# Cross attention in a fused decoder: two layer norms cut into small pieces, and the next row's preparation laid out in thirteen groups

## The chip, the cores and the metric

The kernel runs on one core of a Trainium2 chip. A core has five engines that work side by side, each on its own queue of instructions in a fixed order: TensorE (PE) does matrix products, with its weight loads shown apart (PEld); VectorE (DVE) and ScalarE (ACT) do elementwise work and empty the accumulators (PSUM) that PE writes; GpSimd (POOL) does elementwise work too; SyncE (SP) issues the DMA transfers. An instruction that waits holds up everything behind it on its own queue. The metric is the device time of one execution in microseconds, the median of some runs. The profile is of one execution and has a time of its own.

## The reference

A decoder of two layers on x of 8 batch rows x 512 positions x 256 channels, all float32. Six sublayers follow one another (self attention, cross attention and a local transformer; then quantized attention, media attention and a mixture of experts), each added to its own input's residual. The change touches the second, cross attention with 16 heads of 16 channels:

```python
x = x + _L0_xattn_ref(_layernorm(x), ctx, ctx, adj, mask, Wq, bq, Wk, bk, Wv, bv, Wo, bo)
# in it, per batch row and head: softmax(q k^T / 4 + adj, masked) v, then Wo
...
x = x + _L0_ffn_ref(_layernorm(x), ...)
```

A batch row has 512 queries and 512 keys. `_layernorm` takes mean and variance over the 256 channels of each position and gives (x - mean) / sqrt(var + 1e-5). Two of these norms matter here: the one ahead of cross attention (called x_ln below) and the one ahead of the local transformer (lt_ln), which is worked out at the end of cross attention.

## The kernel before, in words

**Stages.** `fast_stages` runs the sublayers in order on one core. While a stage runs, an `Ahead` object lets the next stage's preparation be written into the program a few pieces at a time (`ahead.step`). The whole of x (`self.x`, 128 partitions x 32 tiles x 256 channels) stays on chip; a batch row is four tiles (`NST`).

**Cross attention** (`stage_cross_attention`, L1476 to L1750) runs a loop over 128 steps, 16 to a batch row; I number rows and steps from 0. A step covers one group of heads and one tile of 128 keys. `scores` (L1640) puts 4 x 2 small products into two PSUM tiles `sc`, of which there are three; `soften` (L1657) takes the exponential of each on ACT (L1663) and multiplies it on DVE by a table `x_share` that holds mask and exp(adj) (L1664); the result is `x_e`, of which there are six buffers, two per step. `weigh` (L1669), two steps behind, multiplies x_e with the values into the PSUM tile `po`, of which there is one. At every fourth step po is copied out by ACT (L1685), its sums of weights go through DRAM and back (`inverted`, L3162), DVE takes their reciprocal (L3174), and a DMA spreads them over the partitions (`x_wide`), where POOL multiplies (L1696).

**The next row's preparation** (`prepare`, L1540) is given out piece by piece with the steps of the current row. In the program's order of before: `load` (three DMA transfers: context, mask, and zeros for a later stage) and `norm` at step 1; `keys` twice at step 2 (K, evicted by DVE at L1601); four `values` (V, evicted by ACT at L1610), with the four `share` pieces (DVE, L1560), at steps 3 to 8; two `turn` (T, transposes, L1578, evicted by ACT at L1581) at steps 9 and 10; two `queries` (Q, evicted by two ACT instructions at L1594) at steps 11 and 12. K, V, T and Q and the final projection all pass through one PSUM tile, `pj`, of which there is one. `norm` is x_ln: per tile bn_stats and bn_aggr (L143, L144), then the mean, the variance and 1/sqrt by a guess and three Newton steps (`rsqrt`, L1455: 12 small instructions together), then four normalizing instructions into `x_xn`, of which there is one (L157), and x + bias on POOL (L1570).

**Work due later.** `Background` holds thunks with a due step; `later.tick(2)` runs at most two of those due in each step. By it the row's projection `project_out` (P, L1709) comes some twelve steps into the next row, four pieces, each a product into pj and an addition into x on DVE (L1717). The fourth also sends the row to DRAM (`away`, L1720) and does lt_ln as a whole: statistics, 12 root instructions, and four normalizing instructions in place on x (lt_ln's L157, LT below).

**What sets the order on the queues.** The kernel is written with Tile, which takes the program's order as a priority and plans a queue for each engine: an instruction is placed when its inputs and its buffers are there, by the planner's own reckoning, and of several that are ready the earliest in the program goes first. So a piece of low priority can stand far ahead of its place in the program when its inputs and buffers are free early. `together` (L1448) keeps the four products of a group side by side on PE.

Of the kernel before, what the change touches and what calls it, by code (L numbers as in the profile page):

```python
# [27 lines left out]
F32 = mybir.dt.float32  # L28
F32R = mybir.dt.float32r
BF16 = mybir.dt.bfloat16  # L30
I32 = mybir.dt.int32
# [3 lines left out]
ALU = mybir.AluOpType  # L35
# [4 lines left out]
P = 128  # L40
B, S, C = 8, 512, 256
NST = S // P
NT = B * NST
EPS = 1e-5
# [12 lines left out]
class Decoder:  # L57
# [1220 lines left out]
class FastDecoder(Decoder):  # L1278
# [177 lines left out]
    def rsqrt(self, pool, out, v, tag):  # L1456
# [4 lines left out]
        for _ in range(3):  # L1461
            nc.vector.scalar_tensor_tensor(t, out, -0.5, out, ALU.mult, ALU.mult)
            nc.vector.tensor_tensor(t, t, v, ALU.mult)
            nc.vector.scalar_tensor_tensor(out, t, 1.5, out, ALU.add, ALU.mult)

    def load_cross_attention(self):
        w = self.weights()
        names = "x_wqT", "x_wkT", "b_wvT", "b_woT"
        return [self.load_w(w, 512 * i, self.t[n]) for i, n in enumerate(names)]
# [6 lines left out]
    def stage_cross_attention(self, ahead):  # L1476
# [6 lines left out]
        nc, t = self.nc, self.t  # L1483
# [41 lines left out]
        bias = self.alloc(pool, [P, C], F32, "x_bias", bufs=1)  # L1525
# [8 lines left out]
        held = {}  # L1534
# [5 lines left out]
        def prepare(b):  # L1540

            d = held[b] = {"v": v_pad[b % 2]}
            own = (first, second)[b % 2]

            def load():
                d["ctxT"] = self.alloc(first, [P, 2, S], F32, "x_ctxT")
                nc.sync.dma_start(
                    d["ctxT"], t["ctxT"].rearrange("(k p) n -> p k n", p=P)[:, :, b * S : (b + 1) * S]
                )
                d["mask"] = self.alloc(first, [P, NST, S], I32, "x_mask", bufs=1)  # L1550
                nc.sync.dma_start(d["mask"], t["x_maskT"][b].rearrange("(k p) q -> p k q", p=P))
                nc.sync.dma_start(
                    self.slots[b * CAP : (b + 1) * CAP, :].rearrange("(p r) c -> p r c", p=P),
                    empty.unsqueeze(1).broadcast_to([P, CAP // P, self.WIDE]),
                )

            def share(k):
                if k == 0:
                    d["share"] = self.alloc(own, [P, NST, S], F32, f"x_share{b % 2}", bufs=1)
                nc.vector.scalar_tensor_tensor(  # L1560
                    d["share"][:, k, :], d["mask"][:, k, :], 0.0, adj[:, k, :], ALU.not_equal, ALU.mult
                )

            def norm():
                x = self.x[:, b * NST : (b + 1) * NST, :]
                stats = self.ln_stats(first, lambda i: [x[:, i, :]], NST, "x_ln")
                d["xn"] = self.alloc(first, [P, NST, C], F32, "x_xn", bufs=1)
                for i in range(NST):
                    self.normalize(d["xn"][:, i, :], x[:, i, :], stats, i)
                nc.gpsimd.tensor_tensor(x, x, bias.unsqueeze(1).broadcast_to([P, NST, C]), ALU.add)  # L1570
                d["xnT"] = self.alloc(first, [P, 2, S], F32, "x_xnT", bufs=1)
                d["q"] = self.alloc(own, [P, 2, 2, S], F32, f"x_q{b % 2}", bufs=1)
                d["k"] = self.alloc(own, [P, 2, S], F32, f"x_k{b % 2}", bufs=1)

            def turn(c):
                ps = self.pj()
                for i in range(NST):
                    nc.tensor.transpose(  # L1578
                        ps[:, i * P : (i + 1) * P], d["xn"][:, i, c * P : (c + 1) * P], self.ident
                    )  # L1580
                nc.scalar.copy(d["xnT"][:, c, :], ps)  # L1581

            def project(wt, src, g):
                ps = self.pj()
                for k in range(2):
                    nc.tensor.matmul(
                        ps, wt[:, k, g * P : (g + 1) * P], src[:, k, :], start=(k == 0), stop=(k == 1)
                    )
                return ps

            def queries(g):
                ps = project(wq, d["xnT"], g)
                for e in range(2):
                    nc.scalar.activation(  # L1594
                        d["q"][:, e, g, :], ps, AF.Identity,
                        bias=qb[:, 2 * e + g : 2 * e + g + 1], scale=qsc[:, e : e + 1],
                    )

            def keys(g):
                ps = project(wk, d["ctxT"], g)  # L1600
                nc.vector.tensor_scalar(d["k"][:, g, :], ps, bk[:, g : g + 1], None, ALU.add)  # L1601

            def values(i):
                ps = self.pj()
                for k in range(2):
                    nc.tensor.matmul(
                        ps[:, :C], d["ctxT"][:, k, i * P : (i + 1) * P], wv[:, k, :],
                        start=(k == 0), stop=(k == 1),
                    )
                nc.scalar.copy(  # L1610
                    d["v"][:, i, :, 1:17], ps[:, :C].rearrange("p (h d) -> p h d", d=16)
                )

            yield load
            yield norm
            for g in range(2):
                yield lambda g=g: keys(g)
            for i in range(NST):
                yield lambda i=i: values(i)
                yield lambda i=i: share(i)  # L1620
            for c in range(2):
                yield lambda c=c: turn(c)
            for g in range(2):
                yield lambda g=g: queries(g)

        second = None
        for thunk in prepare(0):
            thunk()
            yield
        yield Ahead.MAIN  # L1630

        with self.tc.tile_pool(reuse_waits="tile", name="xa", bufs=2) as pool, self.tc.tile_pool(
# [24 lines left out]
            def soften(n):  # L1657
                b, rest = divmod(n, 16)
                kt = rest % 4
                d = held[b]  # L1660
                for p in range(2):
                    ex = self.alloc(pool, [P, 2, 512], F32, "x_e", bufs=6)
                    nc.scalar.activation(ex, d["e"][rest][p], AF.Exp)  # L1663
                    nc.vector.tensor_tensor(  # L1664
                        ex, ex, d["share"][:, kt, :].unsqueeze(1).broadcast_to([P, 2, 512]), ALU.mult
                    )
                    d["e"][rest][p] = ex
# [41 lines left out]
            def project_out(b, i):  # L1709
                ps = self.pj()  # L1710
                for g in range(2):
                    nc.tensor.matmul(
                        ps[:, :C], held[b]["oT", g][:, i * P : (i + 1) * P], wo[:, g, :],
                        start=(g == 0), stop=(g == 1),
                    )
                x = self.x[:, b * NST + i, :]
                nc.vector.tensor_tensor(x, x, ps[:, :C], ALU.add)  # L1717
                if i == NST - 1:
                    rows = self.x[:, b * NST : (b + 1) * NST, :]
                    nc.sync.dma_start(self.away[b], rows)  # L1720
                    stats = self.ln_stats(pool, lambda i: [rows[:, i, :]], NST, "lt_ln")
                    for i in range(NST):
                        self.normalize(rows[:, i, :], rows[:, i, :], stats, i)

            n = 16 * B
            ready = None
            for i in range(n + 2):
                if i < n:
                    if i % 16 == 0:
                        for thunk in ready or ():  # L1730
                            thunk()
                        ready = prepare(i // 16 + 1) if i // 16 + 1 < B else iter(())
                    scores(i)
                    soften(i)
                if i >= 2:
                    weigh(i - 2)

                for _ in range((0, 2, 2, 1, 2, 1, 2)[i % 16] if i % 16 < 7 else 1):
                    thunk = next(ready, None)
                    if thunk is not None:  # L1740
                        thunk()
                later.tick(2)
                if i == 1:
                    ahead.step()
                if i == n - 14:
                    early.close()
                if i >= n - 12:
                    ahead.step(3)
# [1696 lines left out]
```

## Time and profile before

| What | Value |
|---|---|
| Time, median of 3 runs | 3174.21 us (3169.55 to 3178.64) |
| The profiled execution's own time | 3162.05 us |
| Its span, first to last instruction | 3160.1 us |
| Granted TensorE clock over the span | 0.973 |
| Busy over the span: PE, DVE, ACT, POOL | 2877.0, 2166.9, 1154.0, 408.7 us |
| First x_e of cross attention starts, last ends | 207.6, 707.9 us |
| Matmuls of sc (L1652) and po (L1679) | 1024 of 662 ns, 1024 of 620 ns, several at a time |
| x_e: exponential on ACT (L1663), product on DVE (L1664) | 256 of 1026 ns, 256 of 1253 ns |

Groups of instructions are named by line, engine, operation, and output<-inputs by the program's names. Of an instruction, the idle time of its engine just before it and what ended it (its releaser) is given. Matmul ends are modelled, so the starts on PE's timeline are the safer numbers. A line in a helper (L143, L144, L157 and L1455 to L1464) serves several norms; the tile's name tells which.

### The profile page before, as it was taken

Reading aid. Unit: us, or ns where it says so; the run is one execution under the profiler, and the core shown is the slowest. Engines: PE = TensorE matmul, PEld = TensorE weight load, DVE = VectorE, ACT = ScalarE, POOL = GpSimd, SP = SyncE. Lnnn points to the kernel's source line nnn. Section 1 sums busy time; section 2 is a strip of 40 time slices with the busy share of each in tenths; the row PEclk is TensorE's granted clock in tenths of the full one; section 3 lists DMA queues with packets and bytes.
Section 4 is the critical chain, followed back from the end, with each engine's and each line's share of the span. In section 5 each row is a group of like instructions: output and inputs, shape, how many; then the busy total and the mean of one; then the engine's idle time right before and its main releaser. Section 6 shows DMA issues by size and latency. Waiting matters only on the chain. (4 is left out here: it accounts for less than half of the span.)

```text
span 3160.1 us, 40243 instructions
## 1 busy us (share of the span) xinstructions
PE 2877.0 (91%) x14929; PEld 1485.8 (47%) x14944; DVE 2166.9 (69%) x4962; ACT 1154.0 (37%) x1607; POOL 408.7 (13%) x389
## 2 busy tenths in 40 slices
PE   8998888877998989999988989998796999997998
PEld 5642222224555556655555546654444233333665
DVE  7458888887788795357788798558787766566110
ACT  2146556653434431123434431113353444342111
POOL 1111000000011010000101111111201122222111
PEclk9999999989999999999999999999997999998999
DMA  7011111111000001001000011001332122213331
GB/s 237 1 53 44 54 57 48 32 24 51 16 21 22 19 27 42 0 1 35 22 15 21 22 44 61 15 12 60 95 127 94 41 79 103 75 64 103 102 138 59
DMA packets 130695, 168.73 MB, mean 53 GB/s; under 512 B 51760, under 2 KB 79665, under 8 KB 128442
## 3 DMA queue, kind: packets, MB, share of 16 engines
q1 hardware_dynamic: 126394, 154.48, 15.6%
q0 software_dynamic: 4096, 11.59, 1.0%
q8 instruction: 119, 1.95, 0.3%
q14 instruction: 86, 0.70, 0.1%
HBM read 113.12 MB, written 47.50 MB: 51 GB/s over the span
## 5 line engine op out<-in xcount | busy, mean ns | idle before, releaser
L1812 PE MATMUL pj<-w,la_hT 128*128 128x512 f32 x720 | 345.3, 612 | 23.9 <-DVE la_v L1817 21.9
L1664 DVE TENSOR_TENSOR x_e<-x_e,x_share 128x1024 f32<-128x1024 f32 x256 | 309.1, 1253 | 25.1 <-ACT x_e L1663 24.3
L1663 ACT ACTIVATE x_e<-sc 128x1024 f32<-128x1024 f32 x256 | 249.7, 1026 | 147.9 <-PE sc L1652 145.5
L2817 ACT ACTIVATE ma_e<-sc,ma_bias 128x1024 f32<-128x1024 f32 x128 | 142.4, 1114 | 198.8 <-PE sc L2812 185.5
L1812 PEld LDWEIGHTS pj<-w,la_hT 128*128 128x128 f32 x720 | 129.5, 191 | 167.0 <-issue 119.0
L3188 POOL TENSOR_TENSOR la_oT<-la_o,x_wide 128x512 f32<-128x512 f32 x64 | 96.8, 1523 | 790.6 <-DMA x_wide<-invs 654.6
L2825 DVE TENSOR_TENSOR ma_esum<-ma_esum,ma_e 128x1024 f32<-128x1024 f32 x96 | 122.8, 1280 | 91.6 <-ACT ma_e L2817 90.9
L1933 ACT ACTIVATE la_e<-la_e 128x1024 f32<-128x1024 f32 (+1 forms) x128 | 121.4, 951 | 175.2 <-DVE la_e L1929 175.2
L2146 ACT ACTIVATE lf_gate<-pj,lf_b 128x512 f32<-128x512 f32 (+1 forms) x82 | 56.3, 687 | 338.1 <-PE pj L2125 327.1
L1679 PE MATMUL po<-x_e,x_v 128*32 128x512 f32 x1024 | 140.1, 620 | 37.2 <-DVE x_e L1664 34.1
L2125 PE MATMUL pj<-lf_hnT,w 128*128 128x512 f32 (+1 forms) x368 | 171.9, 595 | 1.2 <-DVE lf_hid L2151 1.1
L1929 DVE TENSOR_TENSOR la_e<-sc,la_mask 128x1024 f32<-128x1024 f32 (+1 forms) x128 | 138.3, 1081 | 38.8 <-PE sc L1922 38.8
L1652 PE MATMUL sc<-x_q,x_k 32*128 32x512 f32 x1024 | 159.2, 662 | 0.3 <-ACT x_e L1663 0.2
L2125 PE MATMUL sc<-lf_hnT,w 128*128 128x512 f32 x336 | 158.0, 592 | 0.0
L2197 PE MATMUL po<-w,lf_hid 128*128 128x256 f32 x640 | 148.9, 379 | 0.2 <-DVE x L2207 0.2
L1988 PE MATMUL pj<-w,la_oT 128*128 128x256 f32 x512 | 124.4, 389 | 23.4 <-ACT la_qkT L1858 12.6
L2812 PE MATMUL sc<-ma_qT,ma_kT 64*128 64x512 f32 x512 | 145.2, 644 | 0.0
L2151 DVE SCALAR_TENSOR_TENSOR lf_hid<-sc,lf_b,lf_gate 128x512 f32<-128x512 f32 x70 | 52.4, 748 | 126.3 <-PE sc L2125 126.3
L2835 PE MATMUL po<-ma_e,ma_v 128*64 128x512 f32 x512 | 138.1, 618 | 0.0
L1940 PE MATMUL po<-la_e,la_v 128*64 128x256 f32 (+1 forms) x1024 | 129.1, 374 | 6.4 <-ACT la_o L1962 6.3
L1922 PE MATMUL sc<-la_qkT 64*128 64x256 f32 (+1 forms) x1024 | 132.6, 378 | 1.3 <-DVE la_e L1929 1.3
L1819 ACT ACTIVATE la_sq<-pj 128x512 f32<-128x512 f32 x120 | 71.4, 595 | 156.2 <-PE pj L1812 155.9
(491 smaller groups left out, 5264.5 us busy)
## 6 DMA issues: line engine op xcount, KB each, us to landing
x_wide<-invs SPq DMA_DIRECT2D x184, 128.0 KB
w<-in_f_w_dram SPq DMA_DIRECT2D x16, 1024.0 KB
kv<-kv_o SPq DMA_DIRECT2D x56, 256.0 KB
slots<-x_empty SPq DMA_DIRECT2D x8, 1028.0 KB
x_mask<-in_x_maskT_dram SPq DMA_DIRECT2D x8, 1024.0 KB
ma_kT<-kv SPq DMA_DIRECT2D x8, 1024.0 KB
ma_v<-kv SPq DMA_DIRECT2D x8, 1024.0 KB
ex_rows<-slots SPq DMA_DIRECT2D x7, 1028.0 KB
```

Source lines behind the costliest of these rows:

```text
L1652: nc.tensor.matmul(pair[r // 2][:, r % 2, :], d["k"][rows, g, kt * P : (kt + 1) * P], d["q"][rows, e, g, :], start=True, stop=True,)
L1663: nc.scalar.activation(ex, d["e"][rest][p], AF.Exp)
L1664: nc.vector.tensor_tensor(ex, ex, d["share"][:, kt, :].unsqueeze(1).broadcast_to([P, 2, 512]), ALU.mult)
L1679: nc.tensor.matmul(d["po"][32 * r : 32 * r + 32, :], d["v"][:, kt, 8 * g + 2 * r + e, :], ex[r // 2][:, r % 2, :], start=(kt == 0), stop=( ...
L1812: nc.tensor.matmul(ps, d["hT"][:, k, i * P : (i + 1) * P], wqkv[:, k, j * S : (j + 1) * S], start=(k == 0), stop=(k == 1),)
L1922: nc.tensor.matmul(ps[:, r, jj * 256 : jj * 256 + to - j * P], d["qkT"][rows, 4 + c, j * P : (j + 1) * P], d["qkT"][rows, c, j * P : to], ...
L1929: nc.vector.tensor_tensor(ex[:, :, :n_cols], ps[:, :, :n_cols], mask[:, :n_cols].unsqueeze(1).broadcast_to([P, 2, n_cols]), ALU.add,)
L2125: nc.tensor.matmul(ps[:m, :], w1[:, k, at : at + m], held[b]["hnT"][:, k, :], start=(k == 0), stop=(k == 1))
L2197: nc.tensor.matmul(ps[:, :C], held[b]["hid"][:, f, i * P : (i + 1) * P], w2[:, f, :], start=(f == 0), stop=False,)
L2812: nc.tensor.matmul(ps[:, r, :], d["k"][rows, c, kt * P : (kt + 1) * P], d["q"][rows, c, :], start=True, stop=True,)
L2817: nc.scalar.activation(ex, ps, AF.Exp, bias=bias[:, b * NST + kt : b * NST + kt + 1], scale=0.125)
L2835: nc.tensor.matmul(d["po"][64 * r : 64 * r + 64, :], d["v"][:, kt, 128 * c + 64 * r : 128 * c + 64 * r + 64], ex[:, r, :], start=(kt == 0) ...
```

## The change

Both norms are cut by a new function, `ln_pieces`, which returns three lists of thunks: four for the statistics (one tile each), four for the root (the guess with mean and variance, then three Newton steps), four for the normalization. The instructions are the same as before, in number and size; where they stand in the program is new.

- In `prepare`, thirteen groups replace the single pieces, one group for each of the steps 0 to 12. The loads and the first statistics move from step 1 to step 0; the second K from step 2 to 3; V from steps 3, 4, 6, 7 to 5, 7, 8, 10; share to 4, 7, 9, 12; T from 9, 10 to 8, 9; Q from 11, 12 to 10, 11. POOL's x + bias stands in a thunk of its own (`behind`), after the normalization.
- In `project_out`, each piece takes the statistics of its own tile at once. The root and the normalization of lt_ln become later work: the four root pieces one, two, three and four steps after the last P, the four normalizing pieces five and six steps after it.
- The loop over steps takes one group per step; the list of numbers of pieces by step is gone. Row 0's preparation, which runs during self attention, pauses once a group.

```diff
+    def ln_pieces(self, pool, rows, out, tag):
+        nc = self.nc
+        mv = self.alloc(pool, [P, NST, 2], F32, tag + "_mv")
...
+        def stats(i):
+            st = self.alloc(pool, [P, 1, 6], F32, tag + "_bn", bufs=4)
+            nc.vector.bn_stats(st[:, 0, :], rows[:, i, :])
+            nc.vector.bn_aggr(mv[:, i, :], st.rearrange("p a b -> p (a b)"))
+        def guess():
+            nc.vector.tensor_copy(mean, mv[:, :, 0])
+            nc.vector.tensor_scalar(var, mv[:, :, 1], EPS, None, ALU.add)
+            nc.vector.tensor_scalar(
+                rstd.bitcast(I32), var.bitcast(I32), -0.5, float(0x5F3759DF), ALU.mult, ALU.add
+            )
+        def newton():
+            nc.vector.scalar_tensor_tensor(t, rstd, -0.5, rstd, ALU.mult, ALU.mult)
+            nc.vector.tensor_tensor(t, t, var, ALU.mult)
+            nc.vector.scalar_tensor_tensor(rstd, t, 1.5, rstd, ALU.add, ALU.mult)
+        def normal(i):
+            self.normalize(out(i), rows[:, i, :], (mean, rstd), i)
+        return (
+            [lambda i=i: stats(i) for i in range(NST)], [guess] + [newton] * 3,
+            [lambda i=i: normal(i) for i in range(NST)],
+        )
...
-            def norm():
-                x = self.x[:, b * NST : (b + 1) * NST, :]
-                stats = self.ln_stats(first, lambda i: [x[:, i, :]], NST, "x_ln")
+            x = self.x[:, b * NST : (b + 1) * NST, :]
+            means, roots, normals = self.ln_pieces(first, x, lambda i: d["xn"][:, i, :], "x_ln")
+
+            def behind():
+                nc.gpsimd.tensor_tensor(x, x, bias.unsqueeze(1).broadcast_to([P, NST, C]), ALU.add)
+
+            def rows():
                 d["xn"] = self.alloc(first, [P, NST, C], F32, "x_xn", bufs=1)
-                for i in range(NST):
-                    self.normalize(d["xn"][:, i, :], x[:, i, :], stats, i)
-                nc.gpsimd.tensor_tensor(x, x, bias.unsqueeze(1).broadcast_to([P, NST, C]), ALU.add)
...
-            yield load
-            yield norm
-            for g in range(2):
-                yield lambda g=g: keys(g)
-            for i in range(NST):
-                yield lambda i=i: values(i)
-                yield lambda i=i: share(i)
-            for c in range(2):
-                yield lambda c=c: turn(c)
-            for g in range(2):
-                yield lambda g=g: queries(g)
...
+            yield [load, rows] + means[:2]
+            yield means[2:]
+            yield [roots[0], roots[1], K[0]]
+            yield [roots[2], K[1]]
+            yield [roots[3], M[0]]
+            yield [normals[0], normals[1], V[0]]
+            yield [normals[2], normals[3], behind]
+            yield [V[1], M[1]]
+            yield [T[0], V[2]]
+            yield [T[1], M[2]]
+            yield [Q[0], V[3]]
+            yield [Q[1]]
+            yield [M[3]]
...
+                means, roots, normals = held[b]["norm"]
+                means[i]()
                 if i == NST - 1:
-                    rows = self.x[:, b * NST : (b + 1) * NST, :]
-                    nc.sync.dma_start(self.away[b], rows)
-                    stats = self.ln_stats(pool, lambda i: [rows[:, i, :]], NST, "lt_ln")
-                    for i in range(NST):
-                        self.normalize(rows[:, i, :], rows[:, i, :], stats, i)
+                    nc.sync.dma_start(self.away[b], self.x[:, b * NST : (b + 1) * NST, :])
+                    for k, root in enumerate(roots):
+                        later.add(1 + k, root)
+                    for k, normal in enumerate(normals):
+                        later.add(5 + k // 2, normal)
...
-                for _ in range((0, 2, 2, 1, 2, 1, 2)[i % 16] if i % 16 < 7 else 1):
-                    thunk = next(ready, None)
-                    if thunk is not None:
-                        thunk()
+                for thunk in next(ready, ()):
+                    thunk()
                 later.tick(2)
```

More of the change, by code (lines that the diff above doesn't have):

```diff
@@ L1464, in rsqrt @@
             nc.vector.scalar_tensor_tensor(out, t, 1.5, out, ALU.add, ALU.mult)
+    def ln_pieces(self, pool, rows, out, tag):
+        nc = self.nc
+        mv = self.alloc(pool, [P, NST, 2], F32, tag + "_mv")
+        mean = self.alloc(pool, [P, NST], F32, tag + "_mean")
+        var = self.alloc(pool, [P, NST], F32, tag + "_var")
+        rstd = self.alloc(pool, [P, NST], F32, tag + "_rstd")
+        t = self.alloc(pool, [P, NST], F32, tag + "_t")
+        def stats(i):
[18 more added lines that the diff above has]
+        )
     def load_cross_attention(self):
@@ L1612, in values @@
                 )
-            yield load
-            yield norm
-            for g in range(2):
-                yield lambda g=g: keys(g)
-            for i in range(NST):
-                yield lambda i=i: values(i)
-                yield lambda i=i: share(i)
-            for c in range(2):
-                yield lambda c=c: turn(c)
-            for g in range(2):
-                yield lambda g=g: queries(g)
+            K = [lambda g=g: keys(g) for g in range(2)]
+            V = [lambda i=i: values(i) for i in range(NST)]
+            M = [lambda i=i: share(i) for i in range(NST)]
+            T = [lambda c=c: turn(c) for c in range(2)]
+            Q = [lambda g=g: queries(g) for g in range(2)]
+            yield [load, rows] + means[:2]
[11 more added lines that the diff above has]
+            yield [M[3]]
         second = None
-        for thunk in prepare(0):
-            thunk()
+        for group in prepare(0):
+            for thunk in group:
+                thunk()
             yield
@@ L1717, in project_out @@
                 nc.vector.tensor_tensor(x, x, ps[:, :C], ALU.add)
-                if i == NST - 1:
-                    rows = self.x[:, b * NST : (b + 1) * NST, :]
-                    nc.sync.dma_start(self.away[b], rows)
-                    stats = self.ln_stats(pool, lambda i: [rows[:, i, :]], NST, "lt_ln")
-                    for i in range(NST):
-                        self.normalize(rows[:, i, :], rows[:, i, :], stats, i)
+                if i == 0:
+                    rows = self.x[:, b * NST : (b + 1) * NST, :]
+                    held[b]["norm"] = self.ln_pieces(pool, rows, lambda i: rows[:, i, :], "lt_ln")
+                means, roots, normals = held[b]["norm"]
+                means[i]()
+                if i == NST - 1:
+                    nc.sync.dma_start(self.away[b], self.x[:, b * NST : (b + 1) * NST, :])
[3 more added lines that the diff above has]
+                        later.add(5 + k // 2, normal)
             n = 16 * B
@@ L1729, in stage_cross_attention @@
                     if i % 16 == 0:
-                        for thunk in ready or ():
-                            thunk()
                         ready = prepare(i // 16 + 1) if i // 16 + 1 < B else iter(())
@@ L1736, in stage_cross_attention @@
                     weigh(i - 2)
-                for _ in range((0, 2, 2, 1, 2, 1, 2)[i % 16] if i % 16 < 7 else 1):
-                    thunk = next(ready, None)
-                    if thunk is not None:
-                        thunk()
+                for thunk in next(ready, ()):
+                    thunk()
                 later.tick(2)
```

## The prediction

> **What bounds the kernel now.** I read the page's totals and slices first: TensorE (PE) is busy 2877.0 of 3160.1 us, but the change touches one stage, cross attention, so the averages decide nothing. From the instructions that write x_e (32 per row, 16 steps) I took the rows' starts: 207.6, 264.6, 327.3, 389.5, 453.5, 514.8, 576.8, 634.9 us, the last ending at 707.9. Rows 1 to 6 take 62.7, 62.2, 64.0, 61.3, 62.0 and 58.1 us. Next I cut one period of row 4, whose clock was full throughout, into three stretches where the bound changes (columns: stretch, length, then busy time of PE, PE's weight loads, VectorE (DVE), ScalarE (ACT) and GpSimd (POOL), granted clock, DMA share, GB/s):
>
> ```profile
> 464.20:479.00 14.80, 14.53 (x97) 5.27 (x96) 9.71 (x10) 9.70 (x13) 1.27 (x1) 1.00 0.08 19
> 479.00:491.40 12.40, 11.99 (x81) 3.60 (x76) 11.72 (x15) 10.55 (x14) 1.77 (x1) 1.00 0.25 68
> 491.40:525.50 34.10, 25.12 (x140) 8.37 (x140) 30.62 (x51) 17.91 (x21) 2.17 (x2) 1.00 0.21 64
> ```
>
> Stretch A (steps 4 to 8: second K, four V) is PE's: PE idles 0.3 us, DVE 5.1. Stretch B (steps 9 to 12: two T, first Q) is full on both. Stretch C (step 12 to the next row's step 3) is DVE's: PE idles 9 us, DVE 3.5. Per row DVE works 52.05 us and PE 51.65 of 61.3: neither bounds the row, the row is a sum of stretches with different limits. What PE waits for in C, from the timeline of PE (start, length, last bracket: idle before and releaser):
>
> ```profile
> 513.63 1.07 PE L1679 MATMUL po<-x_e,x_v 128*32 128x512 f32 x8 [2.60 <-DVE x_e L1664]
> 517.32 1.07 PE L1679 MATMUL po<-x_e,x_v 128*32 128x512 f32 x8 [1.56 <-DVE x_e L1664]
> ...
> 523.63 1.98 PE L1586 MATMUL pj<-x_ctxT,w 128*128 128x512 f32 x4 [2.26 <-DVE x_k L1601]
> ```
>
> The first follows the burst of the lt_ln norm; the last is the second K waiting for the single pj bank, whose eviction stands behind x_e on DVE. On DVE, the burst of the x_ln normalization with what POOL does beside it, and the eviction that comes late:
>
> ```profile
> 488.18 1.37 DVE L157 TENSOR_SCALAR x_xn<-x,x_ln_mean,x_ln_rstd 128x256 f32<-128x256 f32 x4
> 490.24 0.25 DVE L3174 RECIPROCAL x_inv<-x_sums 128x16 f32<-128x16 f32 x1 [0.68 <-DMA x_sums<-sums]
> 490.41 3.80 DVE L1664 TENSOR_TENSOR x_e<-x_e,x_share 128x1024 f32<-128x1024 f32 x2
> ...
> 509.92 1.38 DVE L157 TENSOR_SCALAR x<-x,lt_ln_mean,lt_ln_rstd 128x256 f32<-128x256 f32 x4
> ```
>
> One more thing decides how to read the diff: **issue order is not program order.** PE's order follows the program, late only where pj is taken, but DVE's does not. These x_xn are for row 6, while row 4 runs: the planner put them where T of row 5 had freed the one x_xn buffer. All 32 bn_stats of x_ln lie between 37.0 and 250.9 us. The four share pieces, programmed at steps 4 to 8, run in steps 0 and 1. So small DVE pieces go where their inputs and buffers come free, whatever step they are given to; only PE's order, and the priority of ready DVE work against x_e, are really changed.
>
> [...] a 128x4 root piece takes 0.16 us, a 128x256 normalize 0.41; the change adds none. [...] two x_e take 3.80 us beside POOL's x+bias (L1570, 2.35 us) against 2.35 us alone. [...] pj has one bank, and the 2.26 us above are that.
>
> **The change part by part**, per row. Starts in PE's timeline give what a group costs: sc 1.07, po 1.00, K or Q 1.92, V or P (project_out) 1.06, T 0.59 us.
>
> 1. *LT in pieces.* lt_ln's 12 root instructions ran 507.68 to 509.92 (2.24 us), the normals 1.38. By the program the first two root pieces still stand ahead of the x_e of step 15, the third and fourth behind those of steps 15 and 0, the normals at steps 1 to 3. DVE does the same work, in stretch C, where it is the bound; the pieces also stand ahead of the share pieces, which give way. I take 0. Bounds: -1.4 if the normals slide into DVE's idle time in A; +0.4 if the pieces push K's eviction (0.74 us) back.
> 2. *K1 one step later.* It now has a po ahead of it in PE's queue: 1.0 of the 2.26 us is filled. -1.0; between 0 (that po's own x_e is late) and -1.0.
> 3. *V2 and V3 from steps 6, 7 to 8, 10.* Two of 1.06 leave stretch A: -2.1. DVE has 5.1 us of idle there, so PE's saving counts whole; the 2.1 us wait for the sums' DMA at 478.99 can take it back: between 0 and -2.1.
> 4. *V2, V3, and Q1 (step 12 to 11) into B.* PE is full there: 2.1+1.9 = +4.0. ACT's evictions go along (0.39 twice, 1.45): ACT had 10.55 of 12.40, and the longer B takes 2.2 more, so it isn't the bound.
> 5. *Q1 gone from C.* C is DVE's, so PE's 1.9 us count only where DVE waited for PE: the third P came 2.08 us late behind Q1. -2.1; bounds 0 and -2.1.
> 6. *x_xn and POOL's x+bias.* T1 is a step earlier, so the burst (1.38) and the exclusion (3.80-2.35 = 1.45) can run inside the longer B, where DVE now has 4 us to spare, instead of at C's start. Full -2.8, none 0; I take -2.0, the burst whole and under half of the exclusion[...].
> 7. *pj handovers.* T0 to V2 and Q0 to V3 stand in one step, with one sc or po between. After Q0 the next user waited 0.51 us with one sc between (idle before the first P). Two such: +1.0; bounds 0 and +2.
>
> Sum: 0-1.0-2.1+4.0-2.1-2.0+1.0 = -2.2 us a row. Ends: -1.4-1.0-2.1+4.0-2.1-2.8+0 = -5.4, and 0.4+0+0+4.0+0+0+2.0 = +6.4. Rows 1 to 6 have all of it: 6 x -2.2 = -13 us. Row 0 has no P or LT, row 7 prepares nothing: 0.
>
> *Nothing, with its cover.* The three loads of a row (ctxT, mask, zeros into slots) go from step 1 to 0: SP waits for buffers there, not for the step; the mask is used a row later (40 us and more of cover). But the mask load waits on SP for the last share piece, and the sums' DMAs stand behind it: if share came late, DVE's reciprocal would too, and what exceeds A's 5.1 us of DVE idle time would count whole. away stays in the last P; lt_ln normals, which must wait for its read, get more time. By the limit of two thunks a tick, one multiply and one set of four x_wide copies come a step later; their product is wanted only by P, eight steps on. Row 0's preparation, during self attention, has 13 pauses in place of 16 and fits the 21 steps it is given. Rows 6 and 7 are projected after 728 us, and their LT stays one run there.
>
> On the profiled execution (3162.05 us around a span of 3160.1): 3162-13 = 3149. It lay 12 us below the median of the runs, 3174.2, so for the median **3161 us**.
>
> **Rivals.**
> - *It does little* (chance 0.25): the planner fills the same gaps, LT runs in one gap as before, and B's +4.0 eats the rest: within 0 to -1.5 a row, 3165 to 3180, say 3172. For: x_ln already runs a row ahead, and six of seven terms only move work. Against: 3.5 us of PE's waits in C have pj as their cause and their order changes.
> - *PE and pj become the bound in steps 8 to 12: slower* (0.24). T0, V2, T1, Q0, V3, Q1 and four P hand one bank on. [...] It decides from 3.2 us of waits a row, where the gain is gone, and shows as slower from 4.8. For: ACT would have no rest in these steps. Against: T1 followed T0 with no wait above 0.2 us, with an sc and a po between.
> - *DVE never waits* (0.08): pieces fill all its idle time and a row falls to DVE's 52 us plus 3 of DMA waits: -6 a row, -36: 3138. Against: the reciprocal's DMA waits sit in the middle of DVE's order, and each delays x_e behind it.
>
> **How the numbers follow.** My forecast, -8 to -25 us (3149 to 3166), has 0.43. A measurement of this kernel tells about 0.3% from no change, 9.5 us. Faster by that: nearly all of my 0.43 and the 0.08: 0.49. Same: the 0.25 and a little: 0.27. Slower 0.24. The range leaves out half of the two outer cases: 3140 to 3191.
>
> **What would show it.** K1's wait falls from 2.3 to about 1.3 us a row; stretch A shortens to some 12.5 us; the first P's stall and the third P's late arrival shrink; x_xn stands near step 10. Wrong if T's, V's and Q's evictions show as PE waits of over 1 us, if the sums' DMA wait grows past 4 us, or if rows 1 to 6 keep 62 us.

## The result, and the profile after

The changed kernel takes **3143.59 us** (median of 4 runs, 3141.93 to 3154.18) beside 3172.3 us before (median of 4, 3169.55 to 3178.64): ratio **0.9914**, 95% interval 0.9887 to 0.9941. It is faster by 0.9%, or 28.7 us; 13 us were forecast. The profiled execution is the slowest of its four, 3154.18 us around a span of 3152.2, so totals of the two profiles differ by less than the medians do. The stage itself shows the change: from the first x_e to the last it takes 208.0 to 689.3 us, 481.3 us in place of 500.3. From the starts of x_e, rows 0 to 7 take 53.3, 59.9, 60.7, 59.9, 59.9, 59.2, 55.6 and 72.8 us; before they took 57.0, 62.7, 62.2, 64.0, 61.3, 61.9, 58.1 and 73.0.

For one period of a row, I cut the kernel before (row 4) and the kernel after (row 5) at the starts of x_e of the same steps: steps 4 to 7, steps 8 to 13, and step 14 to the next row's step 3. Both periods ran at a full clock. The columns are those of the table of stretches in the prediction; PE, PEld, DVE, ACT, POOL, clock, DMA share, GB/s. First before:

```profile
467.50:481.37 13.87, 13.60 (x92) 4.67 (x88) 10.04 (x10) 10.53 (x14) 1.27 (x1) 1.00 0.14 30
481.37:503.75 22.38, 19.42 (x116) 6.65 (x116) 19.62 (x25) 15.74 (x21) 3.94 (x2) 1.00 0.13 39
503.75:528.81 25.06, 18.64 (x116) 5.93 (x112) 22.39 (x43) 11.90 (x14) 0.00 (x0) 1.00 0.26 80
```

Then after:

```profile
514.66:526.69 12.03, 12.03 (x84) 4.18 (x82) 10.35 (x10) 10.15 (x13) 2.04 (x1) 1.00 0.09 20
526.69:552.51 25.82, 24.84 (x146) 9.05 (x142) 21.39 (x42) 17.75 (x24) 5.68 (x2) 1.00 0.14 43
552.51:572.67 20.16, 14.72 (x90) 4.01 (x92) 19.07 (x26) 10.35 (x13) 0.00 (x0) 1.00 0.08 17
```

The first stretch loses 1.8 us, the second gains 3.4, the third loses 4.9: -3.3 us a row. PE does the same work in both (51.66 and 51.59 us); it stands elsewhere. The third stretch, where PE idled 6.4 us and DVE was the busier, has given away work of both: PE 3.9 us, DVE 3.3 us. The second stretch took up PE's part and 1.8 us of DVE's, and there PE now idles 1 us in place of 3. Over the whole row DVE works 1.2 us less (50.81 us after 52.05); x_e beside POOL's work (below) account for it: three of them took 3.1 us over their usual 1.22 before, two took 1.9 us over it after.

The waits over rows 1 to 6 say the same from the other side (columns: total us, times, longest). PE's before, then after:

```profile
PE po L1679 <- DVE x_e L1664: 25.0, 15, 2.8
PE pj L1712 <- DVE x L1717: 10.4, 5, 2.9
PE pj L1586 <- DVE x_k L1601: 10.1, 5, 2.3
PE pj L1586 <- DVE x L1717: 3.3, 3, 1.5
```

```profile
PE po L1723 <- DVE x_e L1708: 33.1, 18, 2.8
PE pj L1642 <- ACT x_q L1630: 2.8, 6, 0.5
PE pj L1756 <- DVE x L1761: 0.3, 2, 0.2
```

DVE's, before and after:

```profile
DVE x_inv L3174 <- DMA x_sums<-sums: 20.9, 9, 3.4
DVE x_e L1664 <- ACT x_e L1663: 19.2, 16, 1.7
DVE x L1717 <- PE pj L1712: 13.0, 12, 2.1
```

```profile
DVE x_inv L3219 <- DMA x_sums<-sums: 22.4, 14, 2.8
DVE x L1761 <- PE pj L1756: 9.9, 9, 3.0
DVE x_e L1708 <- ACT x_e L1707: 6.4, 8, 1.1
```

What PE waited for the bank pj behind x and x_k, 23.8 us or four a row, is gone but for 0.3 us; 2.8 us behind x_q are new. DVE's waits for x_e (which stand where PE sets the pace, since scores come late there) fall by 12.8 us. The wait of PE for x_e grows by 8: that is idle time where DVE sets the pace, and it costs nothing by itself.

The two norms were not spread over the steps. In row 4 after, the 12 root instructions of lt_ln still run in one gap (between the products of steps 13 and 14), and its four normalizing instructions together one step later. Statistics and root stand about a step earlier, because the four P do: their additions follow the 24th, 25th, 26th and 27th x_e of the row, where they followed the 24th, 26th, 28th and 29th. The root follows the 28th in place of the 30th; the normalizing instructions follow the 30th in both. The burst of x_ln's normalization stands between steps 9 and 10, a step earlier too. On DVE and on POOL, in row 4 after:

```profile
471.33 1.38 DVE L157 TENSOR_SCALAR x_xn<-x,x_ln_mean,x_ln_rstd 128x256 f32<-128x256 f32 x4
472.62 2.35 DVE L1708 TENSOR_TENSOR x_e<-x_e,x_share 128x1024 f32<-128x1024 f32 x2
```

```profile
472.78 4.40 POOL L1603 TENSOR_TENSOR x<-x,x_bias 128x1024 f32<-128x1024 f32 x1 [14.04 <-DVE x_xn L157]
```

and on POOL in row 4 before:

```profile
489.63 2.35 POOL L1570 TENSOR_TENSOR x<-x,x_bias 128x1024 f32<-128x1024 f32 x1 [17.22 <-DVE x_xn L157]
```

Before, POOL's x + bias started first (at 489.63 us) and took 2.35 us, and the two x_e behind it (from 490.41 us) took 3.80. Now x_e starts first, takes 2.35, and POOL takes 4.40. In each trace the one of the two that started first took its usual 2.35 us; the other took 1.45 us more before (the two x_e) and 2.05 us more after (POOL). Nothing waits for POOL here, so the turn is a gain. It shows in rows 4 and 5 alone (4.40 and 4.42 us). In rows 0 to 3 POOL takes 2.35 us in both kernels, and beside it stands a root instruction of x_ln for a later row, `x_ln_rstd`, which takes about 2.35 us in place of the 0.13 to 0.17 that it takes elsewhere.

### The profile page after: what moved, and what is told of

The parts are those of the page before. It is cut to its first block, busy times and chain, and to the rows that moved or that the text cites. A ratio compares the mean times of both kernels' runs of the same rounds, so it can differ in the third digit from the quotient of the medians.

```text
span 3152.2 us, 40259 instructions
## 1 busy us (share of the span) xinstructions
PE 2889.1 (92%) x14944; PEld 1490.9 (47%) x14944; DVE 2169.1 (69%) x4962; ACT 1154.3 (37%) x1607; POOL 412.9 (13%) x389
## 5 line engine op out<-in xcount | busy, mean ns | idle before, releaser
L2033 PE MATMUL pj<-w,la_oT 128*128 128x256 f32 x512 | 124.4, 389 | 23.4 <-ACT la_qkT L1903 12.6
```

## The experiments

The change has two halves, the norms in pieces and the order of the preparation. The first runs take them apart, the next ones take the order apart, the last ones try what waits remain. "Stage" is first to last x_e in the run's own profile. A ratio is to the runs of the kernel before that were taken beside it (9 to 20; 4 for the kernel after), and the 51 runs of the first line are those beside the twelve experiments together. Since runs of one kernel differ with the granted clock (order_only: 3142.62 us at 0.970, 3155.1 at 0.965), the last column gives the time at a mean clock of 0.970 by a straight line through all runs (one slope for all kernels, -1.6 us for 0.001; the runs scatter about it by 2.8 us). It is a reading aid: inv_held, where PE idled 3.72 us at a stretch in row 4, also ran its rows 2 to 6 at a clock of 0.94, where xln_whole, with 2.75 us in row 4, ran them at 1.00 (last section), so the line can take away a part of what a kernel gains or loses.

| Kernel | Median us | Ratio to before, 95% | Stage us | At 0.970 |
|---|---|---|---|---|
| before | 3168.55 (51 runs) | 1 | 500.3 | 3164 |
| after | 3143.59 | 0.9914 [0.9887, 0.9941] | 481.3 | 3148 |
| lt_only | 3166.78 | 0.9995 [0.9983, 1.0008] | 499.3 | 3166 |
| lt_whole | 3145.65 | 0.9928 [0.9909, 0.9948] | 475.5 | 3144 |
| xln_whole | 3143.74 | 0.9928 [0.9908, 0.9947] | 472.6 | 3147 |
| order_only | 3147.24 | 0.9923 [0.9906, 0.9940] | 478.2 | 3146 |
| tq_only | 3158.65 | 0.9953 [0.9935, 0.9971] | 488.8 | 3159 |
| v_only | 3153.34 | 0.9953 [0.9939, 0.9966] | 483.2 | 3151 |
| v_back | 3162.20 | 0.9972 [0.9960, 0.9984] | 490.1 | 3161 |
| tq_back | 3150.84 | 0.9924 [0.9905, 0.9942] | 475.9 | 3145 |
| k1_back | 3153.18 | 0.9951 [0.9933, 0.9969] | 481.7 | 3151 |
| inv_held | 3157.69 | 0.9961 [0.9947, 0.9974] | 491.9 | 3153 |
| inv_due | 3154.67 | 0.9951 [0.9937, 0.9966] | 481.4 | 3152 |
| v3_last | 3143.64 | 0.9929 [0.9913, 0.9945] | 474.8 | 3143 |

### The norms: lt_only, lt_whole, xln_whole, order_only

*lt_only* is the kernel before with `ln_pieces` and the new end of `project_out` (statistics with each P, roots and normals as later work), and nothing else.

```diff
-                    stats = self.ln_stats(pool, lambda i: [rows[:, i, :]], NST, "lt_ln")
-                    for i in range(NST):
-                        self.normalize(rows[:, i, :], rows[:, i, :], stats, i)
+                    for k, root in enumerate(roots):
+                        later.add(1 + k, root)
+                    for k, normal in enumerate(normals):
+                        later.add(5 + k // 2, normal)
```

> The kernel before with the lt_ln norm alone cut into pieces and given out later; the preparation as before. Theory 1 (the order of the users of pj on PE makes the gain, the norm pieces hardly any): the root pieces still run in one stretch, cross attention stays within 494 to 500 us (500.3 before), ratio to before 0.998 to 1.0; PE's waits of the second K and of P stay at about 10 and 14 us over rows 1 to 6. Theory 2 (the lt_ln burst ahead of x_e was the cost): cross attention falls to 481 to 487 us, ratio 0.991 to 0.995.

It changes nothing that can be measured: 0.9995, and PE's waits for pj stay as they were before (a further 2.6 us for x_k stand at V's line, L1641):

```profile
PE pj L1747 <- DVE x L1752: 10.6, 5, 2.9
PE pj L1621 <- DVE x_k L1636: 7.4, 6, 2.3
```

*lt_whole* is the reverse: the kernel after, with the norm whole again in the fourth P (the same lines, the other way round).

> The changed kernel with lt_ln whole again in the fourth P; the thirteen groups stay. Theory 1: nearly all of the gain stays, cross attention 481 to 487 us, ratio to before 0.991 to 0.994. Theory 2: most of it is lost, cross attention 494 us or more, ratio 0.997 or more.

The gain stays, 0.9928. *xln_whole* is the kernel after with x_ln given out as one piece at step 0:

```diff
-            yield [load, rows] + means[:2]
-            yield means[2:]
-            yield [roots[0], roots[1], K[0]]
-            yield [roots[2], K[1]]
-            yield [roots[3], M[0]]
-            yield [normals[0], normals[1], V[0]]
-            yield [normals[2], normals[3], behind]
+            yield [load, rows] + means + roots + normals + [behind]
+            yield []
+            yield [K[0]]
+            yield [K[1]]
+            yield [M[0]]
+            yield [V[0]]
+            yield []
```

> The changed kernel with x_ln in one piece at step 0 (statistics, root, normalization, x+bias together); the other pieces keep their steps. If the planner places these pieces by when x_xn comes free and not by their step, DVE's order in the rows is the same and so is the time: cross attention 480 to 483 us, ratio to the changed kernel within 0.3%. If the steps given to x_ln matter: cross attention 487 us or more.

DVE's order in row 4 is the same as after, instruction by instruction: x_xn follows the 20th x_e in both, though it was programmed at step 0 in the one and at steps 5 and 6 in the other. The stage is 8.7 us shorter than that of the kernel after, which I had not expected; the first K groups that ran slowly in the profile of the kernel after held PE for 6.7 us more than at full clock in rows 0 to 5 (last section), while of rows 0 to 6 of xln_whole only row 1 shows a clock below 1.00 (0.97). *order_only* takes the last step: the kernel before, both norms whole, with the new groups' steps for load, K, V, share, T and Q.

```diff
+            yield [load, norm]
+            yield []
+            yield [K[0]]
+            yield [K[1]]
+            yield [M[0]]
+            yield [V[0]]
+            yield []
+            yield [V[1], M[1]]
+            yield [T[0], V[2]]
+            yield [T[1], M[2]]
+            yield [Q[0], V[3]]
+            yield [Q[1]]
+            yield [M[3]]
```

> The kernel before with the thirteen groups' steps for loads, K, V, T, Q and share, and neither norm cut up. Theory 1 (the order of the users of pj makes the whole gain): cross attention 472 to 484 us, ratio to before 0.991 to 0.994, as the changed kernel. Rival (order and pieces are needed together): 490 us or more, ratio 0.996 or more.

0.9923: the order alone gives the whole gain. Its rows at full clock take 58.1 to 58.2 us, as those of xln_whole (58.0 to 58.1) do. Cutting the norms up gives nothing that can be measured.

### Which part of the order: v_back, tq_only, tq_back, v_only

Two moves of work on PE are left: T and Q one step earlier (1a where the expectations number the theories) or V later (1b). *v_back* is the kernel after with V at its old steps:

```diff
-            yield [roots[2], K[1]]
-            yield [roots[3], M[0]]
-            yield [normals[0], normals[1], V[0]]
-            yield [normals[2], normals[3], behind]
-            yield [V[1], M[1]]
-            yield [T[0], V[2]]
+            yield [roots[2], K[1], V[0]]
+            yield [roots[3], M[0], V[1]]
+            yield [normals[0], normals[1]]
+            yield [normals[2], normals[3], behind, V[2]]
+            yield [M[1], V[3]]
+            yield [T[0]]
...
-            yield [Q[0], V[3]]
+            yield [Q[0]]
```

> The changed kernel with the four V at their old steps 3, 4, 6 and 7; K, T and Q stay. Theory 1a: most of the gain stays, cross attention 475 to 484 us, ratio to before 0.992 to 0.995. Theory 1b: two V of 1.06 us go back into the stretch that PE bounds, 2.1 us a row over seven rows: cross attention 490 us or more, ratio 0.996 or more.

Over half of the gain goes. *tq_only* is the kernel before with T and Q one step earlier and all else at its old step (groups in place of single pieces; only the last share piece comes at step 7 in place of 8, here and in v_only):

```diff
+            yield []
+            yield [load, norm]
+            yield [K[0], K[1]]
+            yield [V[0]]
+            yield [M[0], V[1]]
+            yield [M[1]]
+            yield [V[2], M[2]]
+            yield [V[3], M[3]]
+            yield [T[0]]
+            yield [T[1]]
+            yield [Q[0]]
+            yield [Q[1]]
```

> The kernel before with T and Q alone one step earlier (T at 8 and 9, Q at 10 and 11); K and V at their old steps. Theory 1a (the gain comes from both Q standing ahead of P, so that P's evictions are no longer held up): PE's waits of P fall from 14 us over rows 1 to 6 to under 4, ratio to before 0.993 to 0.996. Theory 1b (the gain comes from V standing later): ratio 0.998 or more.

It has half of the gain; PE's waits behind x fall from 13.7 us to 7.6 over rows 1 to 6, not under 4 as theory 1a had it. *tq_back* is the kernel after with T and Q at their old steps, V late:

```diff
-            yield [T[0], V[2]]
-            yield [T[1], M[2]]
-            yield [Q[0], V[3]]
-            yield [Q[1]]
-            yield [M[3]]
+            yield [V[2]]
+            yield [T[0], M[2]]
+            yield [T[1], V[3]]
+            yield [Q[0]]
+            yield [Q[1], M[3]]
```

> The changed kernel with T and Q at their old steps (T 9 and 10, Q 11 and 12), V at 5, 7, 8 and 10 as changed, but V2 and V3 beside other pieces. Theory 1a: the second Q stands among the P again, PE's waits of P return (10 us or more over rows 1 to 6): cross attention 490 us or more, ratio to before 0.996 or more. Theory 1b: it stays at 472 to 484 us, ratio 0.991 to 0.994.

Nothing that can be measured is lost, against theory 1a, and PE's waits behind x are 4.1 us, not 10. *v_only* is the kernel before with V alone moved to steps 5, 7, 8 and 10:

```diff
+            yield []
+            yield [load, norm]
+            yield [K[0], K[1]]
+            yield []
+            yield [M[0]]
+            yield [V[0], M[1]]
+            yield [M[2]]
+            yield [V[1], M[3]]
+            yield [V[2]]
+            yield [T[0]]
+            yield [T[1], V[3]]
+            yield [Q[0]]
+            yield [Q[1]]
```

> The kernel before with the four V alone moved, to steps 5, 7, 8 and 10; K, T and Q at their old steps, no norm cut up. Theory 3 (two V out of the stretch that PE bounds are nearly the whole gain): DVE's waits for exponentials over rows 1 to 6 fall from 19 us to under 7, cross attention 475 to 485 us, ratio to before 0.991 to 0.995. Rival (V's place only counts together with K's or with the pieces): 490 us or more, ratio 0.996 or more.

Each half alone gives 0.5%, the whole change 0.8%. (Of theory 3, the stage of 483.2 us fits; DVE's waits for exponentials are still 12.4 us, not under 7.) But T's and Q's move isn't needed for the 0.8%: tq_back has V late and the second K a step later, T and Q at their old steps, and 0.9924. What v_only lacks against it (0.9953; the two intervals just touch) would have to come from the second K's step, the loads or the share pieces, since cutting the norms gave nothing; no run takes these three apart beside V. The stretches show how the moves overlap. The same three stretches, for each kernel in one period near full clock (us; rows of one kernel differ, so a difference below 1 us says little here: v_only's rows 2 and 5, at clocks of 0.99 and 1.00, take 60.4 and 58.6):

| Steps | before | tq_only | v_only | v_back | tq_back | after |
|---|---|---|---|---|---|---|
| 4 to 7 | 13.87 | 13.89 | 11.85 | 14.13 | 10.27 | 12.03 |
| 8 to 13 | 22.38 | 24.69 | 21.66 | 23.86 | 22.48 | 25.82 |
| 14 to next 3 | 25.06 | 21.14 | 25.06 | 20.76 | 25.97 | 20.16 |
| sum | 61.31 | 59.72 | 58.57 | 58.75 | 58.72 | 58.01 |

V's move takes 2.0 us out of steps 4 to 7, where PE set the pace, and costs steps 8 to 13 nothing (21.66): PE had 3 us of idle there. T's and Q's move lets the four P and lt_ln go ahead of step 14: steps 8 to 13 grow by 2.3, the last stretch shrinks by 3.9. Together they put both into steps 8 to 13, whose idle time serves only once; so the sum is less than its parts. (v_only's last stretch ran at a clock of 0.86, with PE busy for 21.48 us where before had 18.64, so its own gain is shown a little too small.) tq_back reaches about the same sum another way, with 3.6 us out of the first stretch and 0.9 more in the last. v_back's sum is that of its best row: rows 1 to 5 take 62.4, 60.5, 61.8, 59.7 and 59.6 us, at clocks of 0.94, 0.95, 0.97, 0.97 and 1.00 (in row 4 the first K took 3.16 us; last section).

### The second K: k1_back

The kernel after, second K again in the group of the first.

```diff
-            yield [roots[0], roots[1], K[0]]
-            yield [roots[2], K[1]]
+            yield [roots[0], roots[1], K[0], K[1]]
+            yield [roots[2]]
```

> The changed kernel with the second K back at step 2, beside the first. Theory 1: PE waits again for the eviction of the first K, 1.7 us a row by the kernel before, seven rows with a K: cross attention 490 to 493 us in place of 481.3, ratio to before 0.995 to 0.996. Rival: that wait lies in a stretch that DVE bounds, so that filling it was worth nothing: cross attention stays at 481 to 483 us.

The total can't tell it from the kernel after; the two intervals overlap. PE's wait for x_k did not come back as expected. Over rows 1 to 6 there is one such wait:

```profile
PE pj L1622 <- DVE x_k L1637: 1.1, 1, 1.1
```

This is row 1, the only one of the six at a clock of 1.00, where the first K took its usual 1.98 us. The other five ran at 0.97; in row 3 the first K took 3.56 us (more on that below), which covers the wait. So at full clock the second K's step takes away a wait of 1.06 us. That is one row; tq_only, whose two K stand together as before, has the same wait in all six:

```profile
PE pj L1586 <- DVE x_k L1601: 6.4, 6, 1.1
```

The other half of the 2.26 us of before has another cause: in row 4 before, two share pieces (1.28 us) stood on DVE in the row's first steps, ahead of K's eviction. In row 1 of k1_back and in the rows of tq_only none does: all four come ahead of the row's first x_e. The kernel before has both cases in itself: with all four ahead (rows 0 and 1) the second K waits 1.06 us, with two of them behind the first two x_e (rows 2, 4, 5 and 6) it waits 2.26.

### The reciprocal's wait for the sums: inv_held, inv_due

DVE waits 22 us over six rows for the sums' DMA. Would the kernel gain if the reciprocal stood later? *inv_held* puts it behind the last x_e of the step in which it is due, by an edge in the planned order; *inv_due* makes it due two steps later.

```diff
-                nc.vector.reciprocal(inv, small)
+                with self.tc.issue_after(self.last_product) if held else ExitStack():
+                    nc.vector.reciprocal(inv, small)
```

> The changed kernel with the reciprocal of the sums queued on DVE behind the x_e of the step in which it is due, by an edge of order alone. Theory 3 (a row is now DVE's work of 52 us plus its waits): DVE's waits for the sums' DMA, 22 us over rows 1 to 6, fall under 6, and cross attention to 460 to 470 us, ratio to before 0.985 to 0.989. Rival (PE bounds the row by now, the wait lies beside PE's work): cross attention stays within 472 to 482 us, ratio 0.990 to 0.994.

```diff
-        later.add(3, invert)
-        later.add(5, lambda: then(self.invs[at]))
+        later.add(3 + more, invert)
+        later.add(5 + more, lambda: then(self.invs[at]))
```

> The changed kernel with the reciprocal and what follows it due two steps later, without an edge. If the planner places it by readiness and the due step is only a priority: the reciprocals stand where they stood, DVE's waits for the sums' DMA stay above 18 us over rows 1 to 6, ratio to before 0.990 to 0.994. If the due step counts: the waits fall as with the edge.

Both are slower than the kernel after, against what I expected. In inv_held the wait is gone, and as much has come in its place; DVE's waits over rows 1 to 6 in inv_held:

```profile
DVE x_e L1708 <- ACT x_e L1707: 28.4, 29, 1.9
DVE x L1764 <- PE pj L1759: 12.7, 18, 3.0
DVE x_k L1637 <- PE pj L1622: 7.1, 6, 1.2
```

and in xln_whole, with the reciprocal where the planner puts it:

```profile
DVE x_inv L3219 <- DMA x_sums<-sums: 22.3, 14, 2.9
DVE x L1761 <- PE pj L1756: 9.8, 8, 2.9
DVE x_e L1708 <- ACT x_e L1707: 2.6, 3, 1.1
```

The 22.3 us became 25.8 us more of waiting for ACT's exponentials: DVE stood at the sums where it would have stood for its next x_e anyway. And the row is 3.4 us longer. 1.8 of these are seen in PE: in row 4 the first K takes 3.78 us where xln_whole has 1.98, after an idle stretch of 3.72 us where xln_whole has 2.75. The granted clock of rows 2 to 6 is 0.94 in inv_held, 1.00 in xln_whole. Row 4 in inv_held, after and xln_whole (the line of po, then that of K; the bracket is the idle time before):

```profile
448.21 1.94 PE L1726 MATMUL po<-x_e,x_v 128*32 128x512 f32 x8 [3.72 <-DVE x_e L1708]
450.07 3.78 PE L1622 MATMUL pj<-x_ctxT,w 128*128 128x512 f32 x4
```

```profile
444.23 1.07 PE L1723 MATMUL po<-x_e,x_v 128*32 128x512 f32 x8 [2.76 <-DVE x_e L1708]
445.23 3.44 PE L1622 MATMUL pj<-x_ctxT,w 128*128 128x512 f32 x4
```

```profile
438.95 1.07 PE L1723 MATMUL po<-x_e,x_v 128*32 128x512 f32 x8 [2.75 <-DVE x_e L1708]
439.94 1.98 PE L1622 MATMUL pj<-x_ctxT,w 128*128 128x512 f32 x4
```

Of the other 1.6 us, one lies in steps 14 and 15 (9.34 us where xln_whole has 8.37), where DVE sets the pace and is busy for all of it: with the reciprocal, POOL's multiplication has moved there too (POOL works 1.57 us in these steps, in xln_whole not at all), and DVE is busy for 9.31 us in place of 8.37. The rest I did not settle. In inv_due the reciprocals stand at nearly the same x_e as after, with 17.9 us of waits, but the row's projection comes later and the root pieces of lt_ln fall ahead of the next row's K: PE's waits for x_k are back at 12.6 us and those for x at 11.4.

### One more step the same way: v3_last

The kernel after with the fourth V at the last group.

```diff
-            yield [Q[0], V[3]]
-            yield [Q[1]]
-            yield [M[3]]
+            yield [Q[0]]
+            yield [Q[1]]
+            yield [M[3], V[3]]
```

> The kernel after, with one thing moved on: the fourth V goes from step 10 to step 12, the last group. Theory (the gain is PE's work taken out of stretches where PE is the bound): in steps 10 to 13 PE is still busy for all of the time (10.35 of 10.35 us in a row at full clock), and in steps 14 and 15 it idles 3 of 8.4 us. If V3 falls into the idle part, up to 1.06 us a row goes: stage 466 to 472 us where the best so far had 472.6, ratio to the kernel before 0.990 to 0.992. Rival (in steps 12 to 15 the four P and their adds on DVE set the pace, and V3 only comes ahead of a P on the single pj bank): stage 473 to 479 us, ratio 0.993 to 0.995, and the waits of DVE for P grow from 9.8 us over six rows to 12 or more. Beside it, in both: whether the first K group of each row takes 1.98 us or up to 3.78 us is a matter of the granted clock; it is told apart by that group's length.

Its total lies with the best and can't be told from them. The rows at full clock (4 and 5) take 58.3 and 58.4 us, not the 57 that the first theory wanted; and as the rival says, the bank is waited for again:

```profile
PE pj L1756 <- DVE x L1761: 4.7, 5, 1.6
PE pj L1622 <- DVE x_k L1637: 3.8, 3, 1.3
```

But DVE's waits for P did not grow (8.1 us), so neither theory holds as written. With this placement the row gains nothing more. None of the twelve beats the changed kernel beyond what its intervals leave open.

## Why the prediction was right, and where its sum was not

The case that I held likeliest came true: PE's work is moved out of stretches where PE sets the pace, the waits for pj shrink, and the kernel is faster. 3143.6 us lies inside the range, 17 us below the 3161. How near the sum came is another matter: 28.7 us are more than twice the 13 forecast, 3143.6 lies 4 us from the range's lower end, and the range reaches down that far for a rival's sake (*DVE never waits*), not for the terms'. That the total fell inside is in part luck. By rows: I had -2.2 in rows 1 to 6 and 0 in row 0; at full clock it is -3.3 (row 4 before, row 5 after) and -3.7 in row 0 (both at 0.97). Six times -3.3 and row 0 make -23.5, against -13 (as they ran, rows 1 to 6 of the two profiles differ by 15 us: five slow first K stand in the one after, one in the one before). The 5 us that remain to the medians' -28.7 are inside the interval (19 to 36 us), and the 28.7 may itself be high: the median of the 51 later runs of the kernel before lies 25 us above the kernel after, and the five experiments that keep the gain lie 22 to 27 us below the runs beside them.

- **Issue order is not program order**: right. xln_whole shows it, and lt_only in part (its root still runs in one stretch; three of its four normalizing instructions moved into the next row, without effect). This also carried *LT in pieces, 0* (lt_only: 0.9995).
- *V2 and V3 out of stretch A, -2.1*: right, mechanism and size. v_only has -2.0 in steps 4 to 7, and undoing it alone (v_back) adds 2.1 us there.
- *V2, V3 and Q1 into B, +4.0*: this step failed. I cut B at 491.4 us, where PE was busy for 11.99 of 12.40, and took all that goes in as added. Cut at step 14, PE had 3 us of idle. The two V cost nothing there (v_only 21.66, before 22.38). What lengthens steps 8 to 13 by 3.4 is T's and Q's move, with the P and the lt_ln that follow them (tq_only alone: +2.3). That 3.4 stands near the 4.0 is chance.
- *Q1 gone from C, -2.1*: right in kind, too small. With T and Q alone the last stretch falls by 3.9 us, because not Q1 alone but P and lt_ln leave it too: I moved one product and left what comes behind it in place. What this is worth in the sum is less: 2.3 us come back in steps 8 to 13, and tq_back is as fast without it. The wait that I named hardly changed in the kernel after: DVE waits 9.9 us for P where it waited 13.0. The third P is no longer late, the first one now is, by 2.9 us.
- *K1 one step later, -1.0*: its size is met, as a wait of PE, by one row of k1_back and by six of tq_only, 1.06. The wait fell from 2.3 to nothing and not to 1.3, since two share pieces went out of its way as well. I had named where they run, and not that they delay K's eviction; and in rows 0 and 1 there were only 1.06 us to lose.
- *x_xn and x + bias, -2.0*: the burst stands near step 10 as forecast, and T's step is what moves it: x_xn follows the 20th x_e in tq_only and v_back too, and the 22nd in v_only and tq_back, where T stands at its old steps. What I called the exclusion, the 1.45 us by which two x_e took longer beside POOL, turned round onto POOL (4.40 and 4.42 us in place of 2.35), in two rows of six; I had not forecast that. No run took the time of this term by itself.
- *pj handovers, +1.0*: PE waits 0.47 us once a row for Q's eviction: half.
- *Row 0: 0*: wrong. It has no P and no lt_ln, but K, V, T and Q are moved there as in the others, so I should have given it those terms.

Of the rivals, *PE and pj become the bound, slower* is refuted by the time and by the waits (pj costs PE 6.2 us over six rows, with the 3.1 that were there before as "issue"; its six evictions by ACT, two each of 0.62, 0.39 and 1.45 us, would by my estimate be 4.9 us a row if PE waited for all of them), though PE is busy for 36.87 of the 37.85 us of steps 4 to 13; *it does little* by the interval, though its grounds were good (LT runs in one gap as before); *DVE never waits* by 44 us of DVE's idle time in rows 1 to 6, against 61 before.

## What to carry to other kernels

Where a planner places small work by readiness, cutting it up and dating its pieces may change nothing; look first at the engine whose order does follow the program, and at which of its pieces stand where that engine sets the pace. Cut a period into stretches, price a moved piece by the idle time of the stretch that takes it in, and move with it whatever stands in line behind it. A wait is worth removing only if nothing would be waited for in the next instruction: here removing 22 us of them gained nothing.

## What the runs showed of the hardware

The first K of a row, four products of 128x512, takes 1.98 us or up to 3.78 us, nearly twice as much. Where it was slow, the granted clock was lower too: over steps 2 and 3 of row 4 it was 0.85 in the kernel after (first K 3.44 us) and 0.82 in inv_held (3.78 us), but 1.00 in xln_whole (1.98 us). It goes, loosely, with how long PE idled at a stretch in the 12 us ahead of it:

| Longest idle stretch of PE, us | First K, us | Where |
|---|---|---|
| 3.72 | 3.78 | inv_held, row 4 |
| 2.75 to 2.79 | 2.49 to 3.78 | after, rows 1 to 5; before, row 3; k1_back, row 3; v_back, row 4 |
| 2.75 to 2.76 | 1.98 | after, row 6; k1_back, row 1; xln_whole, row 4 |
| 2.40 to 2.62 | 1.98 to 1.99 | before, rows 2, 4, 5 and 6; tq_back, row 5 |
| 1.26 to 1.74 | 1.98 | before, row 1; tq_back, row 4 |
| 0.99 | 1.98 | before, row 0 |
| 0.99 | 2.55 | after, row 0 |

Equal stretches were followed by both, and row 0 speaks against so simple a rule: in the kernel after, its first K was slow behind nothing longer than 0.99 us. What sets the clock these traces do not show, and no run was made for it.

In the profiled execution after, five slow K cost 0.5 to 1.8 us each in rows 1 to 5, 6.1 us in all (3.65+3.78+2.65+3.44+2.49 less five times 1.98), where the profile of before had one (3.25 us). Executions of these kernels differ by some 10 us; that slow K are a part of this is my reading of single profiles. The same shows behind the stage: of the last eight P, seven take 1.11 to 1.14 us in the profiles of before and after, but the last takes 1.96 us before and 1.84 after, at a granted clock of 0.54 and 0.58, and PE had idled only 1.5 us just ahead of it.
